# Six products with narrow weights, laid side by side in the TensorE array

## The chip, the cores and the metric

The kernel runs on one core of one Trainium2 chip. The metric is the device time of one execution in microseconds (us), lower is better. The kernel before takes 4313.59 us, the median of three runs that lie between 4308.73 and 4316.22 us.

## What is computed

The reference is a network of four layers over 512 nodes of 768 features. Each layer adds a graph network and an attention-like mixer to the residual `x`, and then a feed-forward part. Six products in it have a wide input and only a few columns of output:

- the router of the experts in layers 0 and 2: `logits = xt @ Ws + bs` and `logits = x @ Wg`, 768 features to 8 experts;
- the scores of the experts in layer 3: `scores = sigmoid(x @ gate_weight.T)`, 768 features to 16 experts;
- the attention logits of the graph network of layer 1, which has two convolutions, with three relations and 4 heads, then 1 head;
- the attention logits of the graph network of layer 3, with 12 heads.

Cut to these places:

```python
def _L0_ffn_ref(x, Ws, bs, W1, b1, W2, b2):            # layer 2 alike, with silu and no bs
    logits = xt @ Ws + bs
    probs = jax.nn.softmax(logits, axis=-1)
    routes = jnp.argmax(probs, axis=-1)
    ...                                                # each node through its one expert of 8
def rgat_conv(x, W, q, k, b, src, dst, etype, heads, out_ch, n_nodes):
    xr = jnp.einsum('nd,rdf->rnf', x, W)
    qi = xr[etype, dst] @ q
    kj = xr[etype, src] @ k
    alpha = jax.nn.leaky_relu(qi + kj, NEG_SLOPE)      # then a softmax over the edges of a node
    ...
def _L3_gnn_ref(h, W_fc, attn_l, attn_r, W_res, src, dst):
    ft = jnp.einsum('nhd,ed->nhe', hh, W_fc)
    a1 = jnp.einsum('nhd,hd->nh', ft, attn_l)
    a2 = jnp.einsum('nhd,hd->nh', ft, attn_r)
    ...
def _L3_ffn_ref(hidden_states, gate_weight, Wg, Wu, Wd, Ws_g, Ws_u, Ws_d):
    scores = jax.nn.sigmoid(x @ gate_weight.T)
    topk_score, topk_ids = jax.lax.top_k(scores.T, capacity)   # 64 nodes for each of 16 experts
    ...
```

## The kernel before, in words

All large operands are float32. The 512 nodes lie in four tiles of 128 (`NT`), the 768 features in six chunks of 128 (`KC`). `to_fm` turns an activation from node-major into feature-major form `xnT`, six chunks of 128 features by 512 nodes: 24 TensorE transposes into six PSUM tiles, which VectorE and ScalarE copy out in turn (`copy`, lines 234 and 236). PSUM tiles come from one pool of eight (`ps`). `acc` (line 312) issues a chain of matmuls into one PSUM tile, and `tr` (line 317) a transpose.

Python order is only the order in which work is handed to a scheduler, which fixes the order on each engine's queue ahead of the run; the engines wait for each other by semaphores. The large weights come through one pool `wp` of six buffers of 1152 KB (ten in `ffn3`), filled by DMAs that SyncE issues when a buffer is free (`w`, line 242).

A float32 matmul of the program is two records in the trace, each with its own weight load. So one narrow product, six chunks in a chain, is 12 matmul records of 512 columns. The six places:

- **The two routers**, `moe` for `f0` (layer 0) and `f2` (layer 2). `norm` makes `xn`, `to_fm` makes `xnT`, then the product of `wg`, a piece of the table `cols` of small constants that is loaded once at the start, with `xnT` gives `p[:E]`, logits by expert. VectorE copies them out as `loT` (line 707 or 705), four transposes turn `loT` to node-major, VectorE copies `lo` (line 712). A chain of some forty small VectorE instructions follows (who goes to which expert, into which slot), then indirect DMAs that POOL issues fetch rows and expert weights, and the experts are computed.
- **The scores of layer 3**, in `ffn3`: `to_fm`, product with `gw` (16 columns, also from `cols`), copy `loT` (line 1600), four transposes, sigmoid `sc` on ScalarE (line 1605). Then `rank`, `choose` and `gather` pick 64 rows for each of 16 experts, and the main loop streams 384 weight tiles of 1152 KB: `up` (line 1724) and `down` (line 1740), which already put two experts side by side on 64 columns of the array each.
- **The attention logits of layer 1**, in `rgat`, called twice: product of `V` (24 columns for 4 heads, 6 for 1 head) with `xT`, ScalarE copies `qkT` (line 1126), and the large product of the relation weights starts. Beside it a generator `side` goes on: after the first output tile of the large product, four transposes and a copy `qk` (line 1135), and `parts` (lines 269 to 273), which splits `qkT` into three bfloat16 summands in `qk3`. `V` comes from `fold`, whose matmuls (line 1086) put three relations side by side on 32 columns each.
- **The attention logits of layer 3**, in `gnn3`: product of `V` (24 columns, from `fold3`), copy `qkT` (line 1513), then small products with a block-diagonal `bd`, and after the first node tile of these the transposes, `qk` and `parts`, as in layer 1.

In `counts`, at the start, VectorE builds one-hot matrices of the edges from tiles `worth`, `add` and `so`.

Of the kernel before, what the change touches and what calls it, by code (L numbers as in the profile page):

```python
# [20 lines left out]
P = 128  # L21
# [49 lines left out]
def _thin(w):  # L71

    return np.ascontiguousarray(w.reshape(KC, P, -1).transpose(1, 0, 2)).reshape(P, -1)


def _layout(i):
    a = {}
# [4 lines left out]
    def col(name, m):  # L82
        cols[name] = m
# [25 lines left out]
    for f, n, g in (("f0", "L0_ffn", "Ws"), ("f2", "L2_ffn", "Wg")):  # L109
        col(f + "_wg", _thin(i[f"{n}_{g}"]))  # L110
        a[f + "_w1"] = np.stack([_blocks(w)[0, 0] for w in i[n + "_W1"]])
        a[f + "_w2"] = _rows(i[n + "_W2"])
        a[f + "_b2"] = np.ascontiguousarray(i[n + "_b2"])
        col(f + "_b1", _col(i[n + "_b1"]))
# [30 lines left out]
    a["g3_lr"] = np.ascontiguousarray(np.concatenate([i["L3_gnn_attn_r"], i["L3_gnn_attn_l"]]).T)  # L145
    col("f3_gw", _thin(i["L3_ffn_gate_weight"].T))
    for n in ("Wg", "Wu"):
# [17 lines left out]
class Net:  # L165
    def __init__(self, ctx, tc, dram, at, out):
# [23 lines left out]
        nc.gpsimd.memset(self.bias3, 0.0)  # L190
        self.which = 0
        self.ones = keep.tile([P, P], F32, name="ones")
        nc.gpsimd.memset(self.ones, 1.0)
# [116 lines left out]
    def acc(self, out, pairs):  # L310
        for n, (a, b) in enumerate(pairs):
            self.nc.tensor.matmul(out, a, b, start=n == 0, stop=n == len(pairs) - 1)  # L312

    def tr(self, out, in_):

        k = in_.shape[0]
        self.nc.tensor.transpose(out, in_, self.ident[:k, :k])  # L317
# [45 lines left out]
    def counts(self, c0, g0):  # L363
# [10 lines left out]
        with ExitStack() as c:  # L374
# [13 lines left out]
            worth = one.tile([P, 3, EJ], F32, name="worth")  # L388
            add = one.tile([P, EJ], F32, name="add")
            for n, ((e, u), (f, v)) in enumerate((((3, 0), (3, 1)), ((3, 2), (3, 3)), ((2, 0), (2, 1)))):  # L390
# [290 lines left out]
    def moe(self, f, act, bs=None):  # L681
# [5 lines left out]
        with ExitStack() as c:  # L687
            one = c.enter_context(tc.tile_pool(name=f + "_one", bufs=1))
            two = c.enter_context(tc.tile_pool(name=f + "_two", bufs=2))
            xn = one.tile([P, NT, D], F32, name="xn")  # L690
            xnT = one.tile([P, KC, N], F32, name="xnT")
            self.norm(self.x, xn)
# [6 lines left out]
            xs = self.chunks(xnT)  # L699
            wg = self.col(f + "_wg", 0, KC * E).rearrange("p (k e) -> p k e", k=KC)  # L700
            p = self.ps()
            self.acc(p[:E], [(wg[:, k, :], xs[k]) for k in range(KC)])
            loT = one.tile([E, N], F32, name="loT")
            if bs is None:
                nc.vector.tensor_copy(loT, p[:E])
            else:
                nc.vector.tensor_scalar(loT, p[:E], self.col(bs, 0, 1, E), None, OP.add)
            p = self.ps()
            for t in range(NT):
                self.tr(p[:, t * E : (t + 1) * E], loT[:, t * P : (t + 1) * P])  # L710
            lo = one.tile([P, NT, E], F32, name="lo")
            nc.vector.tensor_copy(lo, p[:, : NT * E].rearrange("p (t e) -> p t e", t=NT))
            m = one.tile([P, NT, 1], F32, name="m")
# [356 lines left out]
    def fold(self, pool, l, H):  # L1070


        nc, d = self.nc, self.d
        wq = pool.tile([P, KC, 32], F32, name="wq")
        nc.gpsimd.memset(wq, 0.0)
        nc.gpsimd.tensor_copy(wq[:, :, : 2 * H], self.col(f"g1_qk{l}", 0, KC * 2 * H).rearrange("p (k h) -> p k h", k=KC))

        def products(temp):
            vt = temp.tile([96, D], F32, name="vt")
            ps = [self.ps() for _ in range(2)]  # L1080
            for kb in range(2):
                ws = [self.wr(d[f"g1_t{l}"][r, kb]) for r in range(3)]
                for j in range(3):
                    for nb in range(2):
                        for r in range(3):
                            nc.tensor.matmul(ps[nb][32 * r : 32 * r + 32, :HW], wq[:, 3 * kb + j, :],
                                             ws[r][:, j, nb * HW : (nb + 1) * HW],
                                             start=kb + j == 0, stop=kb == 1 and j == 2)
            for nb in range(2):
                nc.scalar.copy(vt[:, nb * HW : (nb + 1) * HW], ps[nb][:96, :HW])  # L1090
            return vt

        def turn(V, vt):
            for a in range(2):
                p = self.ps()
                for k in range(3):
                    self.tr(p[:, k * 96 : (k + 1) * 96], vt[:, (3 * a + k) * P : (3 * a + k + 1) * P])
                nc.scalar.copy(V[:, 3 * a : 3 * a + 3],
                               p[:, : 3 * 96].rearrange("p (k r h) -> p k r h", k=3, r=3)[:, :, :, : 2 * H])

        return products, turn

    def rgat(self, xT, l, H, V, C, done, between=None):
# [4 lines left out]
        with ExitStack() as c:  # L1108
# [5 lines left out]
            nc.gpsimd.memset(qk3, 0.0)  # L1114
            qkT = one.tile([J, N], F32, name="qkT")
            mp = c.enter_context(tc.tile_pool(name=f"g1_{l}m", bufs=2))
# [6 lines left out]
            pt = c.enter_context(tc.tile_pool(name=f"g1_{l}p", bufs=BUFS))  # L1123
            p = self.ps()
            self.acc(p[:J], [(V[:, k].rearrange("p r h -> p (r h)"), xT[:, k, :]) for k in range(KC)])
            nc.scalar.copy(qkT, p[:J])

# [3 lines left out]
            def side():  # L1131
                p = self.ps()
                for t in range(NT):
                    self.tr(p[:, t * J : (t + 1) * J], qkT[:, t * P : (t + 1) * P])
                nc.scalar.copy(qk.rearrange("p t r h -> p (t r h)"), p[:, : NT * J])
                self.parts(qk3, qkT, qkT, mid, self.copies, nc.vector.tensor_sub)
                yield
                yield
                for r in range(3):
                    yield from most(r, masks[r])  # L1140
                for _ in ready():
                    yield
                    yield
                yield
                while len(made) < BUFS:
                    for _ in range(2):
                        made.append(next(tiles))
                    yield
# [48 lines left out]
    def gnn1(self, V1, xnT):  # L1197
        nc, tc, d = self.nc, self.tc, self.d
        with ExitStack() as c:
# [32 lines left out]
            with tc.tile_pool(name="g1_ex", bufs=2) as self.elu:  # L1232
                self.rgat(xnT, 1, 4, V1, C, put, between)
            V2 = one.tile([P, KC, 3, 2], F32, name="V2")
            with tc.tile_pool(name="g1_vt", bufs=1) as temp:
# [230 lines left out]
    def fold3(self, one):  # L1466
# [6 lines left out]
        nc.gpsimd.dma_start(lr, d["g3_lr"])  # L1473
        V = one.tile([P, KC, 2 * H], F32, name="V")
        nc.gpsimd.memset(V, 0.0)
# [9 lines left out]
    def gnn3(self, c, xnT, V):  # L1485
# [18 lines left out]
        res = one.tile([P, NT, D], F32, name="res")  # L1504
        qkT = one.tile([2 * H, N], F32, name="qkT")
        qk = one.tile([P, NT, 1, 2 * H], F32, name="qk")
# [3 lines left out]
        pt = c.enter_context(tc.tile_pool(name="g3_pt", bufs=10))  # L1510
        p = self.ps()
        self.acc(p[: 2 * H], [(V[:, k, :], xnT[:, k, :]) for k in range(KC)])
        nc.scalar.copy(qkT, p[: 2 * H])
        for t in range(NT):
# [7 lines left out]
            if t == 0:  # L1522
                q = self.ps()
                for u in range(NT):
                    self.tr(q[:, u * 2 * H : (u + 1) * 2 * H], qkT[:, u * P : (u + 1) * P])
                nc.scalar.copy(qk.rearrange("p t r h -> p (t r h)"), q[:, : NT * 2 * H])
                self.parts(qk3, qkT, qkT, mid, self.copies, nc.vector.tensor_sub)
        yield
# [41 lines left out]
    def ffn3(self, xn, xnT, there):  # L1570
# [5 lines left out]
        with ExitStack() as c:  # L1576
# [7 lines left out]
            first = self.small.tile([P, 1], F32, name="r3")  # L1584
            nc.scalar.activation(first, self.eps, AF.Sigmoid)
            io = one.tile([P, P], F32, name="io")
            nc.gpsimd.iota(io, pattern=[[1, P]], base=0, channel_multiplier=0, allow_small_or_imprecise_dtypes=True)
# [7 lines left out]
            self.to_fm(xn, xnT)  # L1595
            gw = self.col("f3_gw", 0, KC * NX).rearrange("p (k e) -> p k e", k=KC)
            p = self.ps()
            self.acc(p[:NX], [(gw[:, k, :], xnT[:, k, :]) for k in range(KC)])
            loT = one.tile([NX, N], F32, name="loT")
            nc.vector.tensor_copy(loT, p[:NX])  # L1600
            p = self.ps()
            for t in range(NT):
                self.tr(p[:, t * NX : (t + 1) * NX], loT[:, t * P : (t + 1) * P])
            sc = one.tile([P, NT, NX], F32, name="sc")
            nc.scalar.activation(sc, p[:, : NT * NX].rearrange("p (t e) -> p t e", t=NT), AF.Sigmoid)

# [190 lines left out]
def tile_net(ctx, tc, dram, at, out, only=ALL):  # L1797
# [30 lines left out]
    with tc.tile_pool(name="L1", bufs=1) as pool, ExitStack() as keep:  # L1828
# [3 lines left out]
        aT = right.tile([P, KC, N], F32, name="aT")  # L1832
        V1 = pool.tile([P, KC, 3, 8], F32, name="V1")
        products, turn = net.fold(right, 1, 4)
# [47 lines left out]
```

## Time and profile before

| what | value |
|---|---|
| median of three runs | 4313.59 us |
| the profiled execution | 4315.56 us, of which the span of its instructions 4313.8 us |
| mean granted TensorE clock | 0.986 of full speed |
| instructions in the trace | 40131 |
| HBM traffic | 685.09 MB read, 22.54 MB written, a mean of 164 GB/s |
| largest group | line 1724 (`up`), 3072 matmul records, 566.0 us busy |
| narrow product of `f0`, first matmul to copy `loT` | 1229.37 to 1234.72 us |
| narrow product of `f2` | 2820.61 to 2826.29 us |
| narrow product of layer 3's scores | 3172.53 to 3177.89 us |
| narrow products of `rgat`, first and second call | start at 1611.06 and 1793.30 us |
| narrow product of `gnn3` | starts at 2969.66 us |
| stage `ffn3`, its first weight DMA to the end | 3168.83 to 4313.8 us |

In the profile PE is TensorE's matmuls and PEld its weight loads, DVE is VectorE, ACT is ScalarE, POOL is GpSimd, and SP is SyncE, which only issues DMAs here. A letter q behind an engine (SPq, ACTq) marks its instruction queue, as for a DMA that it issues. A timeline row gives start, duration, engine, line, operation, output and inputs, shapes, the count of merged instructions, and in brackets the idle time of the engine before it and what ended it. A busy PE is not a PE at its peak: matmuls overlap, and their ends are modelled.

### The profile page before, as it was taken

To read this page: it belongs to the slowest core of one execution; us is meant where nothing else is said; L and a number is where in the kernel's file an instruction comes from. 1 tells how busy PE (TensorE), PEld (TensorE's weight loads), DVE (VectorE), ACT (ScalarE), POOL (GpSimd) and SP (SyncE) were. 2 spreads that over 40 slices of the span, in tenths; PEclk is the share of its full clock that TensorE was granted. 3 is DMA by queue.
4 is the path that set the end of the run, shared out by engine and by line. 5 is a ranking of instruction groups with operands and counts; after the bars stand their busy time and mean duration, and the time that the engine had idled before them with its cause. 6 is when DMAs were issued, how large, how long until landed. Compare 5 with 4: busy or idle time off the path is not lost. (4 is left out here: it accounts for less than half of the span.)

```text
span 4313.8 us, 40131 instructions
## 1 busy us (share of the span) xinstructions
PE 4125.5 (96%) x16376; PEld 2099.9 (49%) x16376; DVE 1305.0 (30%) x3120; ACT 650.1 (15%) x1233; POOL 270.3 (6%) x316
## 2 busy tenths in 40 slices
PE   7989999999988999999999999978989999999998
PEld 3434555554444666755644444444554444444443
DVE  7772111112332125623220101035752122122211
ACT  2121200001211223421200000012610000000000
POOL 1120000001022010000000000021100000000000
PEclk9999999999989999999999999989999999999999
DMA  3111011111047112211211111063069999999998
GB/s 110 52 62 56 22 44 66 66 55 53 20 178 269 44 63 71 99 52 46 105 43 66 44 56 55 0 255 129 12 257 419 419 420 420 420 417 420 419 421 362
DMA packets 98956, 710.30 MB, mean 165 GB/s; under 512 B 12032, under 2 KB 12097, under 8 KB 29393
## 3 DMA queue, kind: packets, MB, share of 16 engines
q1 hardware_dynamic: 77776, 601.13, 35.1%
q0 software_dynamic: 16512, 93.97, 5.8%
q10 hardware_dynamic: 4480, 12.58, 0.8%
q8 instruction: 132, 2.16, 0.2%
q14 instruction: 56, 0.45, 0.0%
HBM read 685.09 MB, written 22.54 MB: 164 GB/s over the span
## 5 line engine op out<-in xcount | busy, mean ns | idle before, releaser
L1724 PE MATMUL ps<-w,xg 128*64 128x384 f32 x3072 | 566.0, 489 | 4.2 <-DMA w<-in_f_Wg_dram 2.1
L1724 PEld LDWEIGHTS ps<-w,xg 128*64 128x64 f32 x3072 | 234.1, 137 | 296.2 <-issue 271.1
L1356 PE MATMUL ps<-aT,w 128*128 128x512 f32 x864 | 372.3, 592 | 0.0
L1740 PE MATMUL ps<-w,hT 128*64 128x384 f32 x1536 | 320.7, 490 | 7.4 <-DMA w<-in_f_Wd_dram 3.1
L312 PE MATMUL ps<-xnT,w 128*128 128x512 f32 (+1 forms) x732 | 322.6, 598 | 0.2 <-ACT xnT L236 0.2
L1356 PEld LDWEIGHTS ps<-aT,w 128*128 128x128 f32 x864 | 164.2, 190 | 203.6 <-issue 202.3
L360 DVE TENSOR_TENSOR x<-x,ps 128x384 f32<-128x384 f32 x240 | 131.6, 552 | 329.6 <-PE ps L312 259.6
L312 PE MATMUL ps<-w,xnT 128*128 128x384 f32 x672 | 221.7, 486 | 0.2 <-DVE xnT L234 0.2
L312 PEld LDWEIGHTS ps<-xnT,w 128*128 128x128 f32 (+1 forms) x732 | 134.5, 185 | 175.9 <-issue 172.4
L1740 PEld LDWEIGHTS ps<-w,hT 128*64 128x64 f32 x1536 | 131.9, 136 | 170.8 <-issue 145.0
L312 PE MATMUL ps<-w,hT 128*128 128x384 f32 x552 | 189.4, 499 | 8.8 <-ACT hT L850 8.8
L312 PE MATMUL ps<-C,parts 128*128 128x512 bf16 x864 | 188.8, 380 | 2.5 <-DVE inv L1378 2.5
L463 PE MATMUL ps<-ohd,so 128*128 128x512 bf16 x816 | 182.1, 383 | 2.8 <-DVE so L460 2.8
L312 PEld LDWEIGHTS ps<-w,xnT 128*128 128x128 f32 x672 | 127.0, 190 | 88.6 <-issue 4.8
L1366 DVE TENSOR_TENSOR aT<-inv,ps 128x512 f32<-128x512 f32 x72 | 49.4, 686 | 365.7 <-PE ps L312 365.7
L1727 ACT ACTIVATE h<-ps 128x384 f32<-128x384 f32 x64 | 31.4, 490 | 794.0 <-PE ps L1724 794.0
L1728 DVE TENSOR_TENSOR h<-h,ps 128x384 f32<-128x384 f32 x64 | 35.4, 553 | 376.5 <-PE ps L1724 369.3
L312 PEld LDWEIGHTS ps<-w,hT 128*128 128x128 f32 x552 | 105.4, 194 | 83.9 <-ACT hT L850 13.7
L312 PE MATMUL ps<-w,aT 128*128 128x384 f32 (+1 forms) x416 | 139.6, 486 | 0.5 <-DVE aT L234 0.4
L312 PEld LDWEIGHTS <-parts 128*128 128x128 bf16 x864 | 84.8, 98 | 108.1 <-issue 8.8
L312 PE MATMUL ps<-xnT,sw 128*128 128x512 f32 x288 | 136.7, 605 | 0.0
L460 DVE TENSOR_SCALAR so<-io,ind,worth 128x256 bf16<-128x256 int16 x408 | 121.7, 356 | 35.6 <-PE ps L463 35.5
(487 smaller groups left out, 4787.7 us busy)
## 6 DMA issues: line engine op xcount, KB each, us to landing
w<-in_f_Wg_dram SPq DMA_DIRECT2D x128, 1152.0 KB, 14.5
w<-in_f_Wu_dram SPq DMA_DIRECT2D x128, 1152.0 KB, 14.4
w<-in_f_Wd_dram SPq DMA_DIRECT2D x128, 1152.0 KB, 15.2
w<-in_g_w_dram SPq DMA_DIRECT2D x54, 1152.0 KB, 5.1
w<-in_m_wqkv_dram SPq DMA_DIRECT2D x24, 1152.0 KB, 6.7
w<-in_g_t_dram SPq DMA_DIRECT2D x12, 1152.0 KB, 5.6
w<-in_m_wp_dram SPq DMA_DIRECT2D x8, 1152.0 KB, 5.3
ea<-in_edge_attr_dram SPq DMA_DIRECT2D x34, 256.0 KB, 2.7
```

Source lines behind the costliest of these rows:

```text
L312: self.nc.tensor.matmul(out, a, b, start=n == 0, stop=n == len(pairs) - 1)
L360: self.nc.vector.tensor_add(xs, xs, p)
L460: nc.vector.tensor_scalar(so[:, n, :], io[:, h * 256 : (h + 1) * 256], ind[:, 0, j : j + 1], worth[:, n, j : j + 1], OP.is_equal, OP.mult)
L463: nc.tensor.matmul(p, so[:, n, t * P : (t + 1) * P], ohd[:, j, :], start=False, stop=j == (g + 1) * HJ - 1)
L1356: nc.tensor.matmul(outs[nb * 3 + f], w[:, k, f * P : (f + 1) * P], xT[:, k, :], start=first and k == 0, stop=last and k == KC - 1)
L1366: nc.vector.tensor_mul(aT[:, f, :], inv[:, r, :], p)
L1724: nc.tensor.matmul(p[a * 64 : a * 64 + 64, :HW], xg[:, k, a * CAP : (a + 1) * CAP], ws[b][a][:, k, :], start=k == 0, stop=k == KC - 1)
L1727: nc.scalar.activation(h, pg[:, :HW], AF.Silu)
L1728: nc.vector.tensor_mul(h, h, pu[:, :HW])
L1740: nc.tensor.matmul(po[nb][a * 64 : a * 64 + 64, :HW], hT[:, f * P + a * 64 : f * P + a * 64 + 64], wd[a][:, f, nb * HW : (nb + 1) * HW], s ...
```

## The change

The weights of the six products are padded with zeros to 32 columns. `narrow` gives chunk k to the group `32 * (k % 4)` of output partitions: chunks 0 and 4 are summed in partitions 0 to 31, 1 and 5 in 32 to 63, 2 in 64 to 95, 3 in 96 to 127. So a product leaves four partial sums, in one PSUM tile of 128 partitions. `fours` is four 32x32 identities one above the other. Multiplying the four partial sums with it adds them: `narrow_tm` does this with the sums as stationary operand, for each of four node tiles, which adds and turns to node-major form at once; it takes the place of the four transposes. In the three graph places a further product, `fours` against all 512 columns of `qkT`, gives the sum by head that `parts` needs.

Around it: `wg` and `gw` leave the table `cols` (420 columns become 228) and are loaded by DMAs of their own, ACT's for the routers and POOL's in `ffn3`; `V` has 32 columns, and `V1` and `V2` are cleared by POOL first; four small POOL copies build `fours` at the start; `add` in `counts` takes a buffer of the pool of `so`.

```diff
+def _narrow(w):
+    return _thin(np.pad(w, ((0, 0), (0, 32 - w.shape[1]))))
...
-        col(f + "_wg", _thin(i[f"{n}_{g}"]))
+        a[f + "_wg"] = _narrow(i[f"{n}_{g}"])
...
-    col("f3_gw", _thin(i["L3_ffn_gate_weight"].T))
+    a["f3_gw"] = _narrow(i["L3_ffn_gate_weight"].T)
...
+        self.fours = keep.tile([P, 32], F32, name="fours")
+        for i in range(4):
+            nc.gpsimd.tensor_copy(self.fours[32 * i : 32 * i + 32, :], self.ident[32 * i : 32 * i + 32, 32 * i : 32 * i + 32])
...
+    def narrow(self, w, xs):
+        p = self.ps()
+        for k in range(KC):
+            g = 32 * (k % 4)
+            self.nc.tensor.matmul(p[g : g + 32], w[:, k, :], xs[k], start=k < 4, stop=k + 4 >= KC)
+        return p
+
+    def narrow_tm(self, four, n):
+        p = self.ps()
+        for t in range(NT):
+            self.acc(p[:, t * n : (t + 1) * n], [(four[:, t * P : (t + 1) * P], self.fours[:, :n])])
+        return p[:, : NT * n].rearrange("p (t n) -> p t n", t=NT)
...
-            add = one.tile([P, EJ], F32, name="add")
+            add = sp.tile([P, EJ], F32, name="so")
...
+            wg = one.tile([P, KC, 32], F32, name="wg")
+            nc.scalar.dma_start(wg.rearrange("p k e -> p (k e)"), d[f + "_wg"])
...
-            wg = self.col(f + "_wg", 0, KC * E).rearrange("p (k e) -> p k e", k=KC)
-            p = self.ps()
-            self.acc(p[:E], [(wg[:, k, :], xs[k]) for k in range(KC)])
-            loT = one.tile([E, N], F32, name="loT")
+            p = self.narrow(wg, xs)
+            loT = one.tile([P, N], F32, name="loT")
             if bs is None:
-                nc.vector.tensor_copy(loT, p[:E])
+                nc.vector.tensor_copy(loT, p)
             else:
-                nc.vector.tensor_scalar(loT, p[:E], self.col(bs, 0, 1, E), None, OP.add)
-            p = self.ps()
-            for t in range(NT):
-                self.tr(p[:, t * E : (t + 1) * E], loT[:, t * P : (t + 1) * P])
+                nc.vector.tensor_scalar(loT, p, self.col(bs), None, OP.add)
             lo = one.tile([P, NT, E], F32, name="lo")
-            nc.vector.tensor_copy(lo, p[:, : NT * E].rearrange("p (t e) -> p t e", t=NT))
+            nc.vector.tensor_copy(lo, self.narrow_tm(loT, E))
...
-            self.acc(p[:J], [(V[:, k].rearrange("p r h -> p (r h)"), xT[:, k, :]) for k in range(KC)])
-            nc.scalar.copy(qkT, p[:J])
+            p = self.narrow(V, self.chunks(xT))
+            nc.scalar.copy(qkT, p)
...
-                for t in range(NT):
-                    self.tr(p[:, t * J : (t + 1) * J], qkT[:, t * P : (t + 1) * P])
-                nc.scalar.copy(qk.rearrange("p t r h -> p (t r h)"), p[:, : NT * J])
-                self.parts(qk3, qkT, qkT, mid, self.copies, nc.vector.tensor_sub)
+                self.acc(p[:J], [(self.fours[:, :J], qkT)])
+                nc.scalar.copy(qk.rearrange("p t r h -> p t (r h)"), self.narrow_tm(qkT, J))
+                self.parts(qk3, p[:J], qkT[:J], mid, self.copies, nc.vector.tensor_sub)
...
-            V2 = one.tile([P, KC, 3, 2], F32, name="V2")
+            V2 = one.tile([P, KC, 32], F32, name="V2")
+            nc.gpsimd.memset(V2, 0.0)
...
+            gw = one.tile([P, KC, 32], F32, name="gw")
+            nc.gpsimd.dma_start(gw.rearrange("p k e -> p (k e)"), d["f3_gw"])
...
-        V1 = pool.tile([P, KC, 3, 8], F32, name="V1")
+        V1 = pool.tile([P, KC, 32], F32, name="V1")
+        nc.gpsimd.memset(V1, 0.0)
```

`gnn3` and `ffn3` are changed in the same way as `rgat` and `moe`. In the changed program's queues the scheduler keeps the order of everything else, with three shifts that matter below: in `gnn3` the first of the `bd` products comes between the product's chunks 3 and 4; ScalarE's DMA for `wg` stands behind the third `rs` of `norm` in `f0`, and ahead of all of `norm` in `f2`; and POOL clears `V1` just ahead of the `wq` that `fold` waits for.

## What the change was predicted to do

> **What bounds the kernel now.** I read the page's busy times first, then the timeline around each product, then TensorE's waits, then the windows of the weight stream in layer 3.
>
> ```profile
> PE 4125.5 (96%) x16376; PEld 2099.9 (49%) x16376; DVE 1305.0 (30%) x3120; ACT 650.1 (15%) x1233; POOL 270.3 (6%) x316
> DMA  3111011111047112211211111063069999999998
> ```
>
> TensorE is the bound nearly everywhere; in the last eleven of forty slices DMA is full too. Timeline, first router:
>
> ```profile
> 1229.80 4.88 PE L312 MATMUL ps<-xnT,cols 128*8 128x512 f32 x11
> ...
> 1234.72 0.74 DVE L707 TENSOR_SCALAR loT<-ps,cols 8x512 f32<-8x512 f32 x1 [4.22 <-PE ps L312]
> 1235.52 0.32 PEld L317 LDWEIGHTS ps<-ident,loT 8*128 8x128 f32 x4 [1.76 <-DVE loT L707]
> 1235.52 0.41 PE L317 MATMUL ps<-ident,loT 8*128 8x8 f32 x4 [0.83 <-DVE loT L707]
> 1235.97 0.19 DVE L712 COPY lo<-ps 128x32 f32<-128x32 f32 x1 [0.50 <-PE ps L317]
> ```
>
> Here VectorE waits 4.22 us for the product, and all that follows waits for VectorE: the product is latency on the path. In the first rgat it is TensorE time:
>
> ```profile
> 1611.06 5.33 PE L312 MATMUL ps<-xnT,V 128*24 128x512 f32 x12
> ...
> 1616.32 4.14 PE L312 MATMUL ps<-w,xnT 128*128 128x384 f32 x12
> ```
>
> From 1600 to 1830 us TensorE's only listed wait is this, so time taken from its queue is time taken from the stage:
>
> ```profile
> PE ps L317 <- DVE xnT L1229: 0.9, 1, 0.9
> ```
>
> Twelve records take 1616.32 - 1611.06 = 5.26 us, 0.43 each. Do groups of 32 columns really run beside each other? The kernel has two such places, `half` in mix0 (line 547) and `fold` (line 1086):
>
> ```profile
> 394.99 1.06 PE L547 MATMUL ps<-sq,half 96*32 96x512 f32 x6
> 395.98 1.10 PE L312 MATMUL ps<-xnT,w 128*96 128x512 f32 x2
> ...
> 1377.88 0.12 PEld L1086 LDWEIGHTS ps<-w,wq 128*32 128x32 f32 x3 [0.20 <-issue]
> 1378.20 0.12 PEld L1086 LDWEIGHTS ps<-w,wq 128*32 128x32 f32 x3 [0.21 <-issue]
> ```
>
> Six records of three groups give way to the next product after 0.99 us, where one at a time would need 6 x 0.43 = 2.58; and `fold` issues three loads, one for each group, every 0.32 us, the pace of one 384-column record. Three groups overlap fully. Four at once this trace does not show.
>
> Last, the windows of layer 3 (length, then busy time of PE, PEld, DVE, ACT, POOL, then clock, DMA share, GB/s):
>
> ```profile
> 3196.00:3200.00 4.00, 4.00 (x34) 4.00 (x34) 0.56 (x1) 0.00 (x0) 0.00 (x0) 0.91 1.01 414
> 3200.00:3204.00 4.00, 4.00 (x28) 2.06 (x28) 0.00 (x0) 0.48 (x1) 0.00 (x0) 1.00 0.14 55
> 3204.00:3208.00 4.00, 4.00 (x26) 1.73 (x24) 0.00 (x0) 0.49 (x1) 0.00 (x0) 1.00 0.55 180
> 3208.00:3212.00 4.00, 4.00 (x16) 1.89 (x13) 3.17 (x12) 0.00 (x0) 0.00 (x0) 1.00 1.03 430
> ```
>
> The ten weight buffers are full at about 3200, then DMA idles for some 5 us until `up`, which starts at 3200.55, frees two (SyncE's next issue is at 3204.66). After that DMA stays near 420 GB/s. So the stream sets the end, but its gap closes only when TensorE gets through the router: an earlier router still moves the end.
>
> **What the Trainium skill says.** "TensorE: Matmul & The Clock Gate", Part 3 (packing small matmuls), says that outputs at different 32-partition offsets run concurrently, measured 2.38 times faster for three; the trace agrees (2.58 / 0.99 = 2.6). "TensorEngine Tiling (Array Packing)", Key Properties, says that a change of tiling mode drains the engine; I see it as 0.99 against 2 x 0.43 = 0.86, about 0.13 us. "DMA: Bandwidth & Descriptors", Queues, rings and completion order, says that each DMA engine goes round its queues by packets, so a small load behind a weight stream shares with it; in this trace the 384 KB `sw` loads take a median 7.0 us to land, most of them under that stream, and 3.7 at best.
>
> **The product.** New order: four groups with their two records each, 0.86 us, then chunks 4 and 5 in two groups, another 0.86, and 0.2 for two switches: 1.95 us against 5.26, so -3.3 where all six chunks are ready (both rgat calls, gnn3). In the routers chunks 4 and 5 come late: the copies of `xnT` end at about 1230.5 (VectorE, three from 1228.62 in 1.89). Chunk 4's second record then starts at 1230.98, and as VectorE today starts 0.62 after the last record's start (1234.10 to 1234.72), `loT` starts at 1231.6: -3.1. The same sum for f2 (copies end 2821.76; copy out at 2822.85 for 2826.29) gives -3.4, and for layer 3 (3173.68; 3174.77 for 3177.89) -3.1. Copying 128 partitions instead of 8 costs nothing: the 512 columns set the 0.74 us.
>
> **The sum by identities.** Four float32 matmuls are 8 records with loads of 128 columns instead of 4 transposes. Nearest row: `ft<-pt`, 128x65, 32 records in 3.68 us, 0.115 each. So 0.92 for 0.42, +0.5 us at all six places. It is on the path in the routers (`lo` or `sc` waits) and is TensorE time in the graphs. Bounds: 0 if loads hide, +1.0 if each record costs twice that at a low clock.
>
> **The extra product by `fours`** in three places: two records of 512 columns, 0.86 + 0.1 = +0.95 us. `parts` then reads PSUM instead of `qkT`. Its results are first needed by the `sel` products at 2991.07 (gnn3) and 1810.79 (second rgat), 8 to 10 us after the transposes, so its latency is covered; uncovered it would cost about 1 us.
>
> **Loads.** `wg` of f0: ACT's queue reaches it behind `rs` at 1219.12, it waits for attention's space until about 1222.8, as `xn` does, and with a landing of 2.4 us (as for the 96 KB `rf`) it is there at 1225.6, needed at 1229.3. Behind it on ACT is only the store of `xn`, at 1225.32 today. f2: issued after 2807.3, needed at 2820.6. Should it wait for VectorE's last addition (2811.06), the table load and `rs` behind it come some 0.3 us late. Both cost nothing. `gw` is the tight one: POOL can issue it only when TensorE leaves the last products of the mixer (`io`, now at 3168.61, waits for the same), the weight stream starts at 3168.83, and it is needed at 3172.5. Unloaded it lands at 3171.0, at 7.0 us only at 3175.6. Bounds 0 and +3.1; I take +0.3, because its packets are queued before DMA is full (166 GB/s in 3168 to 3172). On POOL it delays `io`, `before` and perhaps SyncE's first weights by 0.55, which the 5 us of idle stream absorb; `before` is not read until 3182.45.
>
> **Small things.** Clearing `V1` (0.27 us, as `wq`) stands ahead of the `wq` for which `fold` waits 6.9 us: +0.27. A `bd` product ahead of chunk 4 in gnn3 waits for loads issued by 2968.69: +0.2. `V2` is cleared among idle POOL work near 1582. The four POOL copies and the smaller `cols` at the start: TensorE waits for `ohd` until 25.5 us, behind VectorE, which waits for `x` until 16.09; I take 0, bounds -0.5 and +0.5. `add` in another pool: same engine, 0.
>
> **Sum.** f0 -3.1 + 0.5 = -2.6; f2 -2.9; layer 3 -3.1 + 0.5 + 0.3 = -2.3; each graph product -3.3 + 0.5 + 0.95 = -1.85, three times -5.55; small things +0.5. Together -12.85 us. The profiled span becomes 4313.8 - 12.85 = 4300.95, its execution 4302.7; from the median, which lies 1.97 below that execution, 4313.59 - 12.85 = 4300.7. I forecast 4300.8. What is late next: in the routers the same VectorE chain, 2.6 us earlier; in rgat TensorE still; in gnn3 the wait for `rows` (3.5 us at 3033.88), which starts from TensorE's own order and moves along; in layer 3 the stream.
>
> **Rivals.** *Part is absorbed.* If DMA sets layer 3 whatever the router does, 2.3 is lost, and if the `rows` wait of gnn3 is fixed by VectorE, 1.85: -8.7, and with `gw` at its upper bound no further, as it is absorbed too: 4304.9. For it: the full DMA. Against: the gap at 3200 to 3208. *Records pair up.* If a group's second record holds up the next group, a product takes seven steps of 0.43 = 3.0 us: 1.1 less gain at six places, -6.3, 4307.3. Against it: three loads per 0.32 us in `fold`. *Groups do not overlap when each streams another chunk*, because four moving inputs at once are more than the array can be fed. Then a product stays at 5.26, and only the additions remain: 6 x 0.5 + 3 x 0.95 + 0.3 + 0.5 = +6.7, 4320.3, plus a drain of 0.13 for each change of group, six a product, +4.7: 4325. It is slower from the point where a product takes more than about 4.3 us. For it: no four at once in the trace; against: `half` and `fold` stream three different inputs at full pace.
>
> **Numbers.** Forecast 0.73, absorbed 0.11, pairing 0.10, no overlap 0.06. What a measurement here can tell from no change is about 0.2%, 8.6 us: faster means below 4305.0. The likeliest case holds 0.70 of that side (its bounds and a spread of 3.7 us in the runs reach past 4305 in 0.03), absorbed about half of its 0.11 and pairing 0.02: faster 0.77. Slower needs the last rival, over 4322.2: 0.05. Same 0.18. The range: 4295 (identities free, start -0.5, spread) to 4308 (pairing).
>
> **What would show it.** Twelve records of each product in about 1.95 us, `loT` 3 us after the first of them, eight records with `fours` in about 0.9 us, `up` starting 12 to 13 us earlier than 3200.55 and the end as much earlier than 4313.8. Wrong if a product still takes over 3 us, if the first matmul of layer 3's router waits for `gw`, or if `up` starts earlier but the end does not.

## The result, and the profile after

| kernel | median, us | ratio to before, 95% interval |
|---|---|---|
| before (in the same comparison) | 4312.43 | |
| changed | 4301.93 | 0.9978 (0.9970 to 0.9986) |

The ratio says 9.5 us (4312.43 x 0.0022), between 6 and 13. The profiled execution took 4306.37 us, 4304.6 of it the span; the profile of before had 4313.8. The page of the changed kernel, its busy times and its line of DMA:

```profile
PE 4112.2 (96%) x16406; PEld 2101.6 (49%) x16406; DVE 1306.5 (30%) x3120; ACT 649.6 (15%) x1233; POOL 273.2 (6%) x323
DMA  3111011111047112211211111063069999999998
```

TensorE has 13 us less work (4125.5 before) with 30 more records, and the digits of DMA are the same. Timeline, first router:

```profile
1226.91 0.14 PEld L328 LDWEIGHTS ps<-xnT,wg 128*32 128x32 f32 x4 [0.48 <-DVE xnT L243]
1226.91 2.25 PE L328 MATMUL ps<-xnT,wg 128*32 128x512 f32 x12 [0.24 <-DVE xnT L243]
...
1229.23 0.75 DVE L731 TENSOR_SCALAR loT<-ps,cols 128x512 f32<-128x512 f32 x1 [1.18 <-PE ps L328]
...
1230.04 1.06 PE L321 MATMUL ps<-fours,loT 128*128 128x8 f32 x8 [0.88 <-DVE loT L731]
1231.13 0.19 DVE L733 COPY lo<-ps 128x32 f32<-128x32 f32 x1 [1.15 <-PE ps L321]
```

Four weight loads, one for each group, are issued in one go. `loT` starts 2.32 us after the first record (5.35 before), `lo` 1.90 after `loT` (1.25 before). In the first rgat (TensorE's rows of the timeline):

```profile
1608.20 1.91 PE L328 MATMUL ps<-xnT,V 128*32 128x512 f32 x12
...
1610.04 4.14 PE L321 MATMUL ps<-w,xnT 128*128 128x384 f32 x12
...
1614.11 1.04 PE L321 MATMUL ps<-qkT,fours 128*24 128x512 f32 x2
...
1615.08 1.07 PE L321 MATMUL ps<-fours,qkT 128*128 128x24 f32 x8
...
1615.99 1.22 PE L321 MATMUL ps<-w,xnT 128*128 128x384 f32 x3
```

From start to start the product takes 1.84 us where one chain took 5.26, so the four groups do run beside each other; the extra product takes 0.97, the eight records of the sum 0.91. Layer 3's router is where it goes wrong:

```profile
3159.55 0.54 POOL L1605 DMA_DIRECT2D gw<-in_f_gw_dram  x1 [17.04 <-PE ps L321]
...
3165.35 2.84 PE L328 MATMUL ps<-xnT,gw 128*32 128x512 f32 x12 [2.33 <-DMA gw<-in_f_gw_dram]
...
3168.23 0.69 DVE L1618 COPY loT<-ps 128x512 f32<-128x512 f32 x1 [3.83 <-PE ps L328]
...
3168.97 1.89 PE L321 MATMUL ps<-fours,loT 128*128 128x16 f32 x8 [0.78 <-DVE loT L1618]
...
3172.51 1.97 PE L341 MATMUL ps<-ident,sc 128*128 128x128 f32 x8 [1.64 <-ACT sc L1620]
```

The product waits 2.33 us for `gw`, and behind the wait the same instructions are slower than elsewhere: 1.89 us for the sum that took 1.06 in the first router, 1.97 for eight transposes that took 1.09 before:

```profile
3180.75 1.09 PE L317 MATMUL ps<-ident,sc 128*128 128x128 f32 x8 [1.64 <-ACT sc L1605]
```

The windows of the changed kernel (TensorE's granted clock is the third figure from the right) show why:

```profile
3163.00:3165.00 2.00, 0.02 (x1) 0.00 (x0) 1.39 (x3) 1.18 (x3) 0.00 (x0) 1.00 0.98 381
3165.00:3167.00 2.00, 1.65 (x10) 0.57 (x12) 0.00 (x0) 0.00 (x0) 0.00 (x0) 0.80 1.04 390
3167.00:3169.00 2.00, 1.22 (x5) 0.03 (x1) 0.69 (x1) 0.00 (x0) 0.00 (x0) 0.50 1.01 415
...
3173.00:3175.00 2.00, 2.00 (x8) 1.61 (x8) 1.09 (x4) 0.00 (x0) 0.00 (x0) 0.50 1.02 433
```

TensorE idles, and from 3166.2 us, within the product, its granted clock is 0.50 for 10.2 us. The weight stream around the start of `up`, in windows of the changed kernel:

```profile
3188.00:3192.00 4.00, 4.00 (x29) 4.00 (x29) 0.56 (x1) 0.00 (x0) 0.00 (x0) 0.74 0.86 359
3192.00:3196.00 4.00, 4.00 (x31) 2.45 (x31) 0.00 (x0) 0.48 (x1) 0.00 (x0) 1.00 0.01 5
3196.00:3200.00 4.00, 4.00 (x28) 1.81 (x26) 0.00 (x0) 0.49 (x1) 0.00 (x0) 1.00 0.38 108
3200.00:3204.00 4.00, 4.00 (x18) 1.90 (x15) 2.49 (x8) 0.00 (x0) 0.00 (x0) 1.00 1.02 431
```

DMA idles some 7 us here, where it idled 5 before: the stream started 9.3 us earlier than before (3159.55 for 3168.83), `up` only 7.2 (3193.30 for 3200.55).

**Stage by stage.** VectorE's instructions come in the same order in all these kernels, so each can be matched with its twin in another trace. The table gives by how much a stage became longer (+) or shorter (-), in us, against a second trace of the kernel before ("again", span 4311.6); its last row is the difference of the spans. Columns are named as in the experiments below.

| stage (time in the second trace of before) | before | changed | changed again | routers_old | graphs_old | f3_old | gw_early | gw_warm | rank_warm |
|---|---|---|---|---|---|---|---|---|---|
| start to 402 | 0.34 | -0.46 | -1.11 | -1.13 | -0.72 | -1.31 | -0.63 | -0.08 | -2.60 |
| mix0, 402 to 428 | 0.00 | -1.69 | 0.00 | 0.00 | 0.00 | 0.00 | -1.69 | -1.69 | 0.00 |
| router f0 to `lo`, 1235 | 0.00 | -2.38 | -2.38 | -0.01 | -2.38 | -2.38 | -2.38 | -2.38 | -2.38 |
| experts f0, second mixer, 1600 | 0.22 | 2.19 | -2.37 | 0.72 | -0.42 | -5.16 | -1.35 | -0.48 | -4.85 |
| rgat, first call, 1628 | 0.00 | -1.91 | -1.91 | -1.91 | 0.00 | -1.91 | -1.91 | -1.91 | -1.92 |
| rgat, second call, 1785 to 1810 | 0.00 | -1.70 | -1.47 | -1.70 | 0.00 | -1.68 | -1.41 | -1.89 | -1.89 |
| to 2806 | -0.05 | -0.16 | -1.14 | 0.07 | -0.12 | 0.54 | -0.04 | -0.23 | 0.56 |
| router f2 to `lo`, 2827 | -0.03 | -2.78 | -2.78 | -1.39 | -2.78 | -3.39 | -2.74 | -2.78 | -3.32 |
| experts f2, 2969 | 0.02 | 2.33 | 1.51 | 0.97 | 2.38 | 1.71 | 2.24 | 2.54 | 0.60 |
| gnn3's product, 3031 | 0.01 | -1.06 | -0.95 | -1.06 | 0.00 | -0.95 | -1.06 | -1.06 | -1.06 |
| gnn3's `rows`, 3051 | -0.03 | -1.23 | -1.23 | -1.23 | 0.14 | -0.14 | -1.23 | -1.24 | -1.24 |
| layer 3, router to ranks, 3181 | 0.00 | 1.50 | 1.02 | 1.12 | -0.25 | 0.00 | -2.39 | 0.04 | -2.04 |
| ranks and gather, 3208 | -0.01 | 0.51 | 0.95 | 0.80 | 0.20 | -0.06 | 0.82 | 1.08 | -1.59 |
| to the end | 1.76 | -0.20 | 0.12 | 0.56 | 0.48 | 0.16 | -0.43 | 0.28 | 0.30 |
| span | 2.20 | -7.00 | -11.70 | -4.20 | -3.40 | -14.60 | -14.20 | -9.80 | -21.30 |

Some rows hardly move between traces of one form (router f0, rgat's first call and gnn3's product by 0.1 us, rgat's second call and router f2 by up to 0.7): these are the change. Others move by 4.6 us between the two traces of the changed kernel (the experts of f0) or step by a fixed amount in some executions and not in others: 1.69 us in mix0, 1.23 in gnn3's `rows`. The second of these steps is the clock. Behind TensorE's wait for `rows`, 3.54 us in every form, the granted clock is 0.50 for 3.41 us where the row has -1.23, and for 6.83 us in both traces of before, in graphs_old, and in f3_old, which has the new gnn3. One pair of traces puts all of this on the change, and so did I in the first expectations below.

### The profile page after: what moved, and what is told of

Read it like the earlier page. It is cut to its first block, busy times and chain, and to the rows that moved or that the text cites. A ratio compares the mean times of both kernels' runs of the same rounds, so it can differ in the third digit from the quotient of the medians.

```text
span 4304.6 us, 40207 instructions
## 1 busy us (share of the span) xinstructions
PE 4112.2 (96%) x16406; PEld 2101.6 (49%) x16406; DVE 1306.5 (30%) x3120; ACT 649.6 (15%) x1233; POOL 273.2 (6%) x323
## 6 DMA issues: line engine op xcount, KB each, us to landing
w<-in_m_wqkv_dram SPq DMA_DIRECT2D x24, 1152.0 KB, 10.8
```

## The experiments

Theory: the six products gain what was forecast, but in layer 3 `gw` lands late, and the idle array then runs at half clock. Rivals: the gains of the routers are given back in the experts' stages; the weight stream sets the end whatever the router does.

**Both kernels once more.** No edit.

> The kernel before once more, for a second trace: it tells which of the differences between the two profiles belong to the change and which to the execution. If they belong to the change, this trace repeats the first one of before: TensorE's eight records rf<-qk in mix0 take 3.45 us (1.99 in the changed kernel), the sel casts of the start 1.97 us (1.09 there), and the last `down` product starts 14 us before the end with a wait of 0.7 us ahead of it. If mix0 and the tail are chance of the clock and of the weight stream, those two differ here by 1 to 2 us and the start does not.

> The changed kernel once more. Theory: the gain of the products (about 12 us at six places) is real, and part of it is given back in layer 3 and behind the two routers; total 4302 us, 10 below before. Repeats for sure: the wait for gw of 2.3 us and the slow identity sum (1.9 us) behind it, start 0.9 earlier, `up` about 7 us earlier than before. Rival: `up` only 7 us earlier was chance of one execution; then this trace has it 10 to 13 us earlier, with a gw wait below 1 us. The step of 1.7 us in mix0 and of 1.8 us in the last 60 us I take for chance: they may be gone.

Before: 4313.36 us, one execution. Changed: 4303.61, ratio 0.9983 (0.9976 to 0.9990), 7 us (4 to 10). The wait for `gw` repeats at 2.3 us, the stage of layer 3 loses 1.97 (2.01 in the first trace), but `up` comes 12.3 us earlier than in the first profile of before, not 7.2: the experts of f0 took 4.6 us less. The step in mix0 is gone. It is the clock; the same line and a window behind it in the first two profiles, before, then changed:

```profile
421.35 3.45 PE L312 MATMUL ps<-rf,qk 97*128 97x256 f32 x8 [0.78 <-DVE qk L234]
...
423.00:425.00 2.00, 2.00 (x6) 1.57 (x5) 0.00 (x0) 1.54 (x4) 0.00 (x0) 0.50 0.00 0
```

```profile
420.55 1.99 PE L321 MATMUL ps<-rf,qk 97*128 97x256 f32 x8 [0.78 <-DVE qk L243]
...
423.00:425.00 2.00, 2.00 (x8) 1.05 (x7) 0.00 (x0) 1.95 (x5) 0.00 (x0) 1.00 0.00 0
```

The wait ahead of it is the same 0.78 us, the code is the same, and 6 of 12 traces of changed kernels have the short form. "TensorE: Matmul & The Clock Gate" of the Trainium skill, Part 1 (The HAM clock gate), says that the array runs at half or full clock by its activity in a window of about 3.4 us that runs free of the program. The traces agree: 0.50 and 1.00 are the only levels. In the eight traces with the long form, two of them of before, the clock is at 0.50 for one stretch of 3.41 us; in the other six, after the same pause, it has not fallen. And every stretch at half clock in the 14 traces, but for the one that ends each trace, is a multiple of 3.41 us long.

**`gw` early, in two ways.** In the first the buffer is kept, and the scheduler, free to place the load, issues it at 0.7 us of the run. In the second `gw` is a piece of `cols`.

```diff
+        self.gw = keep.tile([P, KC, 32], F32, name="gw")
...
+            if f == "f2":
+                nc.scalar.dma_start(self.gw.rearrange("p k e -> p (k e)"), d["f3_gw"])
...
-            gw = one.tile([P, KC, 32], F32, name="gw")
-            nc.gpsimd.dma_start(gw.rearrange("p k e -> p (k e)"), d["f3_gw"])
+            gw = self.gw
```

> gw loaded in layer 2 into a buffer that is kept, so that the product of layer 3 waits for nothing. Theory A (late gw and a cold array): the wait of 2.3 us goes, and with it the low clock that followed it (identity sum 1.9 -> 1.06 us, eight transposes 1.97 -> 1.09, first shared product 6.4 -> 5.3); `up` starts 4 to 4.5 us earlier than in the changed kernel, and since SyncE's issues keep the distance to `up` to 0.01 us through the main loop, the end is 4 us earlier too: 4298. Theory B (the weight stream sets the end from its own start): `up` is earlier, the idle time of DMA shrinks, the end stays within 0.5 us: 4302. Theory C (the clock is low for another reason): only the wait goes, 2.3 us: 4299.6 with the identity sum still at 1.9.

```diff
-    a["f3_gw"] = _narrow(i["L3_ffn_gate_weight"].T)
+    col("f3_gw", _narrow(i["L3_ffn_gate_weight"].T))
...
+            gw = self.col("f3_gw", 0, KC * 32).rearrange("p (k e) -> p k e", k=KC)
```

> gw, padded, as a piece of the table cols, which has 420 columns again as before the change; wg stays apart. In layer 3 it must do the same as gw_early (3.6 us less than the changed kernel). At the start it tells why the changed kernel is 0.7 to 1.9 us earlier there: theory S1 (the smaller table: the rows that POOL's queue loads behind it land 0.9 us sooner, so POOL's work on them no longer stands beside VectorE's sel casts): the row lands near 18.7 us again, sel casts take 1.97 us, and the start gains nothing against before. Rival S2 (POOL's four copies for fours shift POOL's other work): the start stays 0.9 us or more earlier than before. Total 4297 with S2, 4298 with S1.

gw_early: 4296.99 us, ratio 0.9969 (0.9957 to 0.9981). gw_cols: 4299.82, 0.9975 (0.9965 to 0.9985). TensorE's timeline of gw_early in layer 3:

```profile
3159.90 2.24 PE L329 MATMUL ps<-xnT,gw 128*32 128x512 f32 x12 [0.24 <-DVE xnT L244]
3163.05 1.04 PE L322 MATMUL ps<-fours,loT 128*128 128x16 f32 x8 [0.91 <-DVE loT L1620]
3165.73 1.34 PE L342 MATMUL ps<-ident,sc 128*128 128x128 f32 x8 [1.64 <-ACT sc L1622]
...
3178.43 8.01 PE L322 MATMUL ps<-oh,xn 128*128 128x128 f32 x48 [4.77 <-DVE oh L1648]
```

The wait is gone and the sum takes 1.04 us. Up to the ranks the stage gains 2.39 us (gw_cols 2.16), where the changed kernel loses 1.0 to 1.5; up to `up` it is 3.6 us shorter than in the changed kernel (-2.39 + 0.82 against 1.50 + 0.51). Theory B, the stream, falls: the first weight DMA is 12.6 us earlier than in the first trace of before, `up` 14.2, and SyncE's issues stay at 14.2 (all but one within 0.03) for a thousand microseconds, as they stay at 7.2 in the changed kernel. Not all of theory A came: the shared product still took 6.8 us at a falling clock, and the gather of expert rows, the last line, starts cold.

At the start gw_cols, with 420 columns again, came near what S1 expected: at 24 us it is 0.29 us ahead of the second trace of before (the two traces of the changed kernel 0.96 and 1.19, the first trace of before 0.04), its row lands at 18.44 us and its `sel` casts take 1.80, as this timeline shows:

```profile
18.44 0.81 POOL L278 CAST bias<-row 1x768 bf16<-1x768 f32 x1 [6.54 <-DMA row<-in_m_bv_dram]
20.16 1.80 DVE L193 CAST sel<-ident 32x32 bf16<-32x32 f32 x3
```

In the changed kernel the row came at 17.77 and the casts took 1.09. But by 402 us gw_warm, which has the small table, has gained only 0.08 us, and others 0.5 to 2.6. What the start is worth beyond some 0.5 us stays open.

**The clock alone.** Ten matmuls of an identity that nobody reads keep TensorE busy while `gw` is awaited.

```diff
+    def warm(self, n):
+        p = self.ps().rearrange("p (a b) -> p a b", a=4)
+        for _ in range(n):
+            self.nc.tensor.matmul(p, self.identb, self.identb[:, None, :].to_broadcast([P, 4, P]), start=True, stop=True)
...
+            self.warm(10)
             p = self.narrow(gw, self.chunks(xnT))
```

> The changed kernel with ten bfloat16 matmuls that nobody reads, issued on TensorE just ahead of layer 3's product, so that the array is busy while gw is awaited. Theory A1 (the wait of 2.3 us for gw costs twice, once itself and once more because TensorE's clock falls to half in it): the wait stays, but the clock behind it is 1.0 instead of 0.5, the identity sum takes 1.06 us instead of 1.9, eight transposes 1.1 to 1.3 instead of 1.97, and `up` comes 1.3 to 1.6 us earlier behind layer 3's first instructions than in the changed kernel (there the stage loses 2.0 us against before, three times out of three). Rival A2 (the clock is no part of it): the stage still loses 2.0 us.

4300.94 us, ratio 0.9979 (0.9971 to 0.9987). TensorE's timeline:

```profile
3163.73 1.91 PE L334 MATMUL ps<-xnT,gw 128*32 128x512 f32 x12 [1.57 <-DMA gw<-in_f_gw_dram]
3166.44 1.07 PE L321 MATMUL ps<-fours,loT 128*128 128x16 f32 x8 [0.79 <-DVE loT L1625]
3169.14 1.09 PE L347 MATMUL ps<-ident,sc 128*128 128x128 f32 x8 [1.64 <-ACT sc L1627]
```

`gw` lands no sooner, and all three are at full clock. The half clock comes later, in the shared product that follows. At the ranks the stage is at +0.04 us: 1.5 less than the first trace of the changed kernel (the clock) and 2.4 more than gw_early (the wait). graphs_old, below, shows the same by chance: its clock held through a wait of 2.33 us and through the sum, and it stands at -0.25:

```profile
3170.37 1.91 PE L328 MATMUL ps<-xnT,gw 128*32 128x512 f32 x12 [2.33 <-DMA gw<-in_f_gw_dram]
3173.07 1.06 PE L321 MATMUL ps<-fours,loT 128*128 128x16 f32 x8 [0.79 <-DVE loT L1622]
```

**One part undone.** In each the named places have the one chain and the four transposes again; in f3_old `gw`, with 16 columns, is a piece of `cols` again too. The cut shows the product of routers_old.

```diff
-            p = self.narrow(wg, xs)
+            p = self.ps()
+            self.acc(p[:E], [(wg[:, k, :E], xs[k]) for k in range(KC)])
```

> The two routers of layers 0 and 2 have the one-chain product and the four transposes again; the graphs and layer 3 stay changed. If a router's gain stays on the path as predicted (2.6 and 2.9 us), this is 5.5 us slower than the changed kernel: 4307.5. If most of it is given back in the expert stage (gathers that land late, weights that land late), as the first pair of traces suggests with 0.5 us left behind f0 and 0.6 behind f2, it is only 1 us slower: 4303, with the logits 2.5 us later but the xnT copies behind each expert stage within 1 us of the changed kernel's.

> The three graph products go back to the old form (one chain with the first columns of the padded V, four transposes, no product by fours); routers and layer 3 stay changed. The traces show 1.9, 1.4 to 1.9 and 2.3 us gained at the three places, so this is 5.9 us slower than the changed kernel, 4308.5, with the offsets of rgat and gnn3 against before at 0 within 0.3 us. If the graph gains were absorbed by waits that follow (the `rows` wait in gnn3), the offset behind gnn3 would be within 1 us of the changed kernel's and the total 4304.5.

> Layer 3's scores alone go back to the old form: one chain of 12 records, 16 columns of gw from the table cols, four transposes; routers of layers 0 and 2 and the graphs stay changed. If the change of layer 3 as it was made costs time (the stage from its first weight DMA to `up` lost 1.9 to 2.0 us against before in three traces), this is 2.0 us faster than the changed kernel, 4300.5, and the offset against before stays constant from 3169 us to `up`. The prediction's own reading (layer 3 gains 2.3 us) would have it 2.3 us slower: 4305.

| kernel | median, us | ratio to before, 95% interval |
|---|---|---|
| routers_old | 4308.76 | 0.9995 (0.9987 to 1.0003) |
| graphs_old | 4308.19 | 0.9992 (0.9984 to 1.0001) |
| f3_old | 4302.86 | 0.9980 (0.9973 to 0.9987) |

Without the routers the gain shrinks from 7 us (changed again, the same comparison) to 2, as the sum of two router gains says; what the first pair of traces seemed to give back behind f0 was chance, since that row runs from +2.2 to -5.2 for kernels with the same router. Behind f2 some is given back: 1.5 to 2.5 us in most traces of the new form (0.60 in rank_warm), 0 in both of before. But routers_old, with the old router, has 0.97, so how much of it is the product's stays open. graphs_old has 0.00 in both rgat rows and in gnn3's product, and its total is near the 4308.5 that was expected. f3_old loses nothing in layer 3: the change there cost 2.0 us, as expected, where the prediction has a gain (1.9 in routers_old, nothing in graphs_old, whose clock held); its total is too close to the changed kernel's to show it.

The -1.39 of routers_old at router f2 is no gain of the product. TensorE's line ahead of it, first changed, then routers_old, differs by the clock:

```profile
2808.75 5.35 PE L341 MATMUL ps<-ident,xn 128*128 128x128 f32 x24 [5.89 <-issue]
```

```profile
2810.90 4.12 PE L341 MATMUL ps<-ident,xn 128*128 128x128 f32 x24 [5.89 <-issue]
```

**Three groups.** `g = 32 * (k % 3)`, sums from 96 partitions.

> The changed kernel with three groups of two chunks instead of four (two groups of two, two of one); the sums come from 96 partitions. Working of the prediction: four chunks side by side, then two, is 0.86 us twice; three and three is 0.86 us twice as well. So the product takes 1.84 us in rgat as before, within 0.1, and the time is that of the changed kernel, 4302 to 4303. If instead the groups share the feeding of the array (each further stream costs), three side by side are faster than four: 1.7 us or less. If the fourth group is worth something, the product takes over 2.0.

4303.17 us, ratio 0.9983 (0.9976 to 0.9989). Its product in the first rgat:

```profile
1607.96 1.92 PE L328 MATMUL ps<-xnT,V 128*32 128x512 f32 x12
```

The next product starts 1.85 us later: three groups of two chunks are as fast as four.

**Warm arrays elsewhere.** On top of gw_early: warm_moe has 43 unread matmuls in each router, all_warm 18 more ahead of layer 3's gather, rank_warm only these 18.

```diff
             nc.vector.tensor_copy(wayT, p)
+            self.warm(22)
...
             shared(0, 0)
+            self.warm(18)
             choose(0)
```

> gw_early with 43 bfloat16 matmuls that nobody reads in each of the two routers, in TensorE's idle times between the logits and the first expert, where its clock is 0.5 for some 20 us. Theory W (the shorter product leaves the first expert a colder array: its 12 records take 6.3 us in layer 2 against 5.15 in the kernel before and 4.14 at full clock): they take 4.14 us in both routers, the stages behind the routers of layers 0 and 2 are each 1 to 2 us shorter than in gw_early, total 4293.5. Rival: the first expert waits for its gathered weights, so a faster array only waits longer: the copies of xbT move by less than 0.5 us, total 4297. If a matmul nobody reads stands in the way of the gather's transposes, it is slower by up to 1 us a router.

> warm_moe with 18 more matmuls that nobody reads, in layer 3, between the first shared product and the gather of expert rows (`oh`, xn), where TensorE waits 4.8 us for VectorE's ranks. In gw_early the gather's 48 records start at half clock and take 8.0 us, in the kernel before 7.2. If it is the clock, they take 5.3 to 5.6 here, `up` starts 2.4 us earlier behind the ranks, and the end follows: 4293. If they are bound by something else (loads of 128 columns), they stay at 7 to 8 us: 4295.7.

> gw_early with the 18 matmuls that nobody reads ahead of layer 3's gather alone, none in the routers: it tells whether those in the routers are worth their place. all_warm had the gather at 5.6 us instead of 8.0, and `up` earlier by 1.6 us behind the ranks than its own offset at the ranks; that must repeat here. If the 43 matmuls in each router bring nothing (medians of gw_early and warm_moe 1.3 us apart, intervals that overlap), this has the time of all_warm, ratio 0.9962 within 0.001, some 16 us below before. If they bring 1 to 2 us each, it is 2 to 4 us slower than all_warm: ratio 0.997.

| kernel | median, us | ratio to before, 95% interval |
|---|---|---|
| warm_moe | 4295.74 | 0.9967 (0.9955 to 0.9979) |
| all_warm | 4296.43 | 0.9962 (0.9949 to 0.9976) |
| rank_warm | 4295.64 | 0.9964 (0.9950 to 0.9978) |

The routers' 43 bring nothing that can be measured. In f2 the first expert still took 5.83 us (6.25 in the changed kernel, 5.15 before), and in f0, at 4.14, the next product waited 0.96 for weights. Ahead of the gather the 18 do what was expected; rank_warm's timeline, to be held against the last line of gw_early:

```profile
3172.99 5.60 PE L322 MATMUL ps<-oh,xn 128*128 128x128 f32 x48 [1.24 <-DVE oh L1654]
```

8.01 us became 5.60, and from ranks to `up` the stage turns from +0.82 to -1.59 us. Against gw_early's total the difference is inside the intervals. rank_warm, 15 us below before, is the kernel I would keep.

## Why the prediction was right

The forecast of 4300.8 us met 4301.93, and the mechanism at five of the six places is as forecast. That the time came so close is in part luck. The gain was forecast at 12.85 us and measured at 9.5 (6 to 13) and 7 (4 to 10) in two comparisons, and in the first of them the kernel before ran 1.2 us below the median from which the forecast started. One term was wrong by 4.3 us.

- *The product*, forecast at 1.95 us: 1.84 in rgat. In the routers `loT` was to come 3.1 (f0) and 3.4 (f2) earlier behind the first record: 3.03, and 3.40 (2816.31 - 2814.03 against 2826.29 - 2820.61). Layer 3 with `gw` in time: 2.39 gained although the sum costs 0.66, so 3.05, for 3.1.
- *The sum by identities*, +0.5: 0.91 us of TensorE, as the 0.92 taken from `ft<-pt`, but +0.65 to `lo`.
- *The product by `fours`*, +0.95: 0.97.
- *By place*: f0 -2.38 for -2.6; f2 -2.78 for -2.9; rgat -1.91, and -1.41 to -1.89, for -1.85 each. gnn3 -1.06 for -1.65: the `bd` pair ahead of chunk 4 cost more than 0.2. Product and pair take 3.11 us (2962.65 to 2965.76), 2.65 without the pair's usual 0.46, so 0.7 above 1.95:

```profile
2962.65 1.56 PE L328 MATMUL ps<-xnT,V 128*32 128x512 f32 x8 [0.33 <-DVE xnT L243]
2964.15 0.70 PE L321 MATMUL ps<-bd,xnT 128*128 128x256 f32 x2
2964.78 1.05 PE L328 MATMUL ps<-xnT,V 128*32 128x512 f32 x4
2965.76 2.43 PE L321 MATMUL ps<-bd,xnT 128*128 128x256 f32 x10
```

- *The step that failed*: "I take +0.3, because its packets are queued before DMA is full". POOL and SyncE issued at the same moment, 3159.55; POOL's instruction alone takes 0.54 us, and DMA is full two and a half microseconds later (a share of 1.04 in the window from 3162). In five further traces the load took 5.6 to 6.4 us to land. It is not POOL's queue alone: `rf`, 96 KB on the same queue with little else on DMA, landed in 2.4 to 2.5. The wait of 2.3 us lies within the bounds of the prediction, but they were bounds on the wait alone: the half clock behind it cost another 1.0 to 1.5 (the two traces of the changed kernel at the ranks against gw_warm's 0.04), and the gather, colder with `gw` in time too, 0.5 to 1.0. Layer 3 came to +2.0 for -2.3.
- *Small things*: `wg` cost nothing, as said. Clearing `V1` cost 0.14 for 0.27: from the start of VectorE's last `x` to `fold`'s first matmul it is 2.44 us, within 0.01, in the twelve traces of changed kernels and 2.30 in both of before. That a product would make the kernel slower from about 4.3 us on is off a little: 1.95 + 12.85 / 6 is 4.1.
- *What is late next*: as forecast. The wait for `rows` is 3.54 us in both forms, and SyncE's issues follow `up` to the end of the stream; only its last 60 us vary, by 2. `up` was 7.2 us earlier in one trace and 12.3 in the other, for 12 to 13.
- *Rivals*: no overlap and pairing fall with 1.84 us, absorption by DMA with gw_early. Nor does the wait for `rows` absorb gnn3's gain: the changed kernel is 7.60 us ahead of the second trace of before on both sides of it.

Measured by place, -2.38 - 2.78 - 1.91 - 1.70 - 1.06 + 2.01 = -7.8 us, against 9.5 and 7 in two comparisons. With `gw` in time it is -11.4, and gw_early and gw_cols measure 13.4 and 10.8. The sum leaves out the 1.23 of `rows`, the clock's, and what is given back behind f2.

## What to carry to other kernels

When a small operand leaves a table that was loaded long ago, its own load must be issued well ahead of any weight stream, or it lands in the stream's time. Price a new idle time of TensorE twice: the wait, and the half clock of what may follow it (it followed in four of the five traces with a wait of 2.3 us and an array that nothing kept busy). And take a second trace of the unchanged kernel before giving a stage's few microseconds to a change.

## What the runs showed of the hardware

- Four groups of 32 columns, each streaming its own float32 chunk of 512 columns, ran fully beside each other: 12 records in 1.84 us, for 5.26 in one chain; three groups in 1.85.
- Behind a pause of 0.8 us on TensorE, the same in every trace, the clock fell to half for 3.41 us in 8 of 14 traces, which cost 1.69 us, and did not fall in the other 6.
- Every stretch at half clock, but for the one that ends each trace, lasted a multiple of 3.41 us. Behind the same wait of 3.54 us the new gnn3 had 6.83 us of it in one kernel (f3_old) and 3.41 in the others, a difference of 1.1 us in the time.
- 96 KB took 1.9 us to land with little else on DMA (`wg`, from ACT's queue; 2.4 to 2.5 for `rf`, from POOL's) and 5.6 to 6.4 beside the start of the weight stream (`gw`, from POOL's).
